# The last 96-row tile of gate and up: from seven products of 96 rows to seven of 64 rows and a plain 32 + 32, in 64-column matmuls

## The chip, the cores and the metric

The kernel runs on one core of a Trainium2 chip. Its engines each work through their own queue: TensorE (PE in the profile; its weight loads are shown as PEld), VectorE (DVE), ScalarE (ACT), GpSimd (POOL) and SyncE (SP), which issues most of the DMA transfers. The metric is the device time of one execution in microseconds (us); lower is better. Before the change it is 2099.88 us, the median of three runs (2099.81 to 2101.02).

## The reference

The input x has 8 batches of 1024 tokens with 512 features, all in float32. The tokens are normalised, and two branches are computed from them; their product is added to x.

```python
xn = _layernorm(x, axis=-1)
s = _L0_attn_ref(xn, ...)          # three decayed retrievals, gated, 128 wide
gate = einsum('bsh,oh->bso', xn, lut[gate_idx])     # 512 -> 1376
up   = einsum('bsh,oh->bso', xn, lut[up_idx])       # 512 -> 1376
h    = silu(gate) * up
g    = silu(einsum('bsh,oh->bso', h, lut[down_idx]))  # 1376 -> 512
return x + s * g
```

The weights of gate, up and down come from a table of 16 values by integer indices. 1376 = 10 x 128 + 96, so that gate and up have a last tile of 96 rows. The change concerns this tile.

## The kernel before, in words

**Two phases.** Phase 1 (`phase_1`) normalises and transposes the tokens, computes the retrieval branch batch by batch, and builds the weights from the indices on the side. It writes what phase 2 needs to device memory: the weights, already with the sums that the products below need, and for each batch in `xs_d` the transposed tokens and their sums. Phase 2 (`phase_2`) runs over the 8 batches. For each it computes h with the products of gate and up (`quads` for ten tiles, `single` for the last), and then `down`.

**Seven products for eight.** Gate and up are multiplied in blocks of two by two. The 1024 tokens of a batch form two halves: quarters 0 and 2 are one, quarters 1 and 3 the other. The 512 features form two halves too, and gate and up stand one over the other. Instead of eight block products there are seven, on sums and differences of weight blocks (s1 to s4) and of token blocks (t1 to t4). The products' results are combined by copies in PSUM and by additions. Token blocks are b11 and b21 (first token half, first and second feature half), b12 and b22 (second token half). Products 1 to 3 use b11, b21 and b22 themselves, products 4 to 7 sums. b12 itself is used by no product.

**The stage `single` (L831).** Product k has two matmuls (L845), one for each 128 features, with 96 columns of weights and 512 tokens. It uses four PSUM banks: pc (s21), pb (s12), pa (s11) and pe (sE). They show as `fs` and `fsE` in the profile. The order is:

- product 1 into pa; ScalarE copies pa to u2 (L855)
- product 6 into pb; VectorE adds: u2 = pb + u2 (L857), the first addition
- `at_last(5)`: five sums for the stage that follows
- ScalarE copies u2 into pc (L859)
- product 5 into pe; ScalarE copies pe to e (L861)
- product 2 onto pa; ScalarE takes Silu of it (L863)
- product 7 onto pc; VectorE adds: u3 = pc + e (L865), the second addition
- `at_last(1)`: one more sum
- product 3 onto pe; VectorE and ScalarE make Silu of pe + u2 (L868, L869)
- product 4 onto pc; VectorE multiplies by the first Silu (L871); GpSimd multiplies the other half (L872)

The temporary tile t, with u2, u3, e and the Silu, lies in the room "u2" of the pool `tmp` in batch 0, and in the room "e5" of `tmp2` in the others.

**The order around it.** In batch 0 `single` comes before `quads`. There the hook `at_last` is `sums_beside`, which has GpSimd make sums of tokens (L828). In batches 1 to 7 `single` comes after `quads` and before `down`, and `at_last(n)` calls `vector_sums` (L1119, L1123): n of the sums of blocks of h that `down` needs for its first nodes, on VectorE. Ten are planned: four of 128 x 512 into z, four of 128 x 1024 and two of 128 x 512 into sx and sy.

**`quads`** works in nodes (`Node`, L874): two groups of four tiles with seven nodes each, then three nodes for the last pair of tiles, (1, 6), (5, 7) and (2, 3), and `Fourth` (L926), the fourth products of the last pair. Each node loads its weights into one of three ring buffers. After the node (4, 4) of a group, GpSimd multiplies h by a tile u3 and then by a tile e5 (`multiply`, L992 to L994). `restore` (L965) loads the second quarter of a token block again where sums have overwritten it.

**Queues.** `keep_order` ties the instructions of PE, DVE, ACT and POOL to the order of the source, engine by engine. SyncE's order comes from the scheduler; a load that waits for its room holds up those behind it on that queue.

**Phase 1's part.** `features` (L485) writes the token blocks of a half batch to `xs_d` (L520, L525, L531), and `gate_up` (L257) builds a tile's weights: three index loads, a look-up on VectorE, four sums on GpSimd, and a write.

Of the kernel before, what the change touches and what calls it, by code (L numbers as in the profile page):

```python
# [9 lines left out]
F32 = mybir.dt.float32  # L10
# [38 lines left out]
def recurrent_block(ctx: ExitStack, tc, x, wq, wk, wv, wo, wg, decay_logits, out_scale, lut, gidx, uidx, didx, out):  # L49
# [38 lines left out]
    small = p_a = p_c = p_r = None  # L88


    wgu_d = [dram.tile([P, 14, m], F32, name=f"wgud{o}", tag=f"wgud{o}") for o, (_, m) in enumerate(OCH)]
# [154 lines left out]
    def ffn_weights(build, pool, pair_pool):  # L246
# [10 lines left out]
        def gate_up(o):  # L257
            s, m = OCH[o]
            n = 2 * NV * m
            idx = build.tile([P, NB], I32, name="idx", tag="idx", bufs=2)  # L260
            iv = idx[:, :n].rearrange("p (a b) -> p a b", b=m)
# [7 lines left out]
            w = wf[:, : 2 * n].rearrange("p (k two m) -> p k two m", two=2, m=m)  # L269
            a21, a11, a12, a22, s1, s2, s3, s4 = (w[:, k] for k in range(8))  # L270
# [4 lines left out]
            nc.gpsimd.tensor_tensor(s4, a12, s2, ALU.subtract)  # L275
            wide = wf[:, 2 * m : 2 * n].rearrange("p (a b) -> p a b", b=m)
            if o >= 4 * NQ:
                defer(3, lambda: nc.sync.dma_start(out=wgu_d[o], in_=wide))
            if o >= 2 * NK:
                return  # L280
# [106 lines left out]
    def project(b, pools, sides, kept):  # L387
# [97 lines left out]
        def features(hf):  # L485
# [48 lines left out]
            nc.scalar.copy(c11, pa)  # L534
# [254 lines left out]
    W_OF = {1: 0, 2: 1, 4: 2, 5: 3, 6: 4, 7: 5, 3: 6}  # L789
    X_OF = {1: 0, 2: 1, 3: 2, 5: 3, 6: 4, 7: 5, 4: 6}  # L790
    D_OF = {1: 0, 7: 1, 2: 2, 3: 3, 5: 4, 6: 5, 4: 6}
    ORDER = (1, 6, 5, 7, 2, 3, 4)

    def phase_2():
        with (
# [18 lines left out]

                return fx.tile([P, 7, 7, H], F32, name=f"xs{b}", tag="xs")

            def load_x(b, xs, first=0, end=7):
                nc.sync.dma_start(
                    out=xs[:, first:end, 0:4, :],
                    in_=xs_d[b][:, 2 * first : 2 * end].rearrange("p (k r) (s t) -> p k (r s) t", r=2, s=2),  # L820
                )

            def sums_of_x(xs):
# [4 lines left out]
                    nc.gpsimd.tensor_tensor(o, x1, x2, ALU.subtract)  # L828
                    yield

            def single(b, o, xs, h_tail, at_last, room):  # L831

                s, m = OCH[o]
                w = ring.tile([P, 14, P], F32, name=f"wr{b}_{o}", tag="wr")
                nc.sync.dma_start(out=w[:, :, :m], in_=wgu_d[o])
                ha, hb = h_tail[:m, :U], h_tail[:m, U:]


                pc, pb, pa, pe = (bank(r, f"f{r}{b}_{o}")[:m, :] for r in ("s21", "s12", "s11", "sE"))
                t = room.tile([P, 4, U], F32, name=f"t{b}_{o}", tag="e5" if room is tmp2 else "u2")  # L840
                u2, u3, e, sg = (t[:m, k, :] for k in range(4))

                def product(ps, k, start, stop):
                    for n in range(2):
                        nc.tensor.matmul(  # L845
                            ps,
                            lhsT=w[:, 2 * W_OF[k] + n, :m],
                            rhs=xs[:, X_OF[k], 2 * n : 2 * n + 2, :],
                            start=start and n == 0,
                            stop=stop and n == 1,  # L850
                            skip_group_check=True,
                        )

                product(pa, 1, True, False)
                nc.scalar.copy(u2, pa)  # L855
                product(pb, 6, True, True)
                nc.vector.tensor_tensor(u2, pb, u2, ALU.add)  # L857
                at_last(5)
                nc.scalar.copy(pc, u2)  # L859
                product(pe, 5, True, False)  # L860
                nc.scalar.copy(e, pe)  # L861
                product(pa, 2, False, True)
                nc.scalar.activation(sg, pa, AF.Silu)  # L863
                product(pc, 7, False, False)
                nc.vector.tensor_tensor(u3, pc, e, ALU.add)  # L865
                at_last(1)
                product(pe, 3, False, True)
                nc.vector.tensor_tensor(hb, pe, u2, ALU.add)  # L868
                nc.scalar.activation(hb, hb, AF.Silu)  # L869
                product(pc, 4, False, True)  # L870
                nc.vector.tensor_tensor(ha, pc, sg, ALU.mult)  # L871
                nc.gpsimd.tensor_tensor(hb, hb, u3, ALU.mult)  # L872

            class Node:  # L874

# [81 lines left out]
                def fifth_copy(self):  # L957
                    self.add()

            def quads(b, xs, h, sums, made, at_last):  # L960

                def restore(*ks):  # L965

                    some_of = slice(X_OF[ks[0]], X_OF[ks[-1]] + 1, max(X_OF[ks[-1]] - X_OF[ks[0]], 1))
                    there = xs_d[b].rearrange("p (k r) t -> p k r t", r=2)
                    nc.scalar.dma_start(out=xs[:, some_of, 1, :], in_=there[:, some_of, 0, H:])

                def two(ap):
                    return ap.rearrange("p (a t) -> p a t", a=2)
# [86 lines left out]
                def every():  # L1059
                    for q in range(NQ):  # L1060
                        for ks, empty, after in steps(q):
                            yield Node(b, q, ks, xs), empty, after
                    for ks, empty, after in pair_steps():
# [304 lines left out]
            more = iter(())  # L1368
            xs = room_for_x(0)
            for k in (1, 6, 5, 2, 7, 3, 4):  # L1370
                load_x(0, xs, X_OF[k], X_OF[k] + 1)
            for b in range(B):
                h = hp.tile([P, 2 * NK, T], F32, name=f"h{b}", tag="h")
                h_tail = hp.tile([P, T], F32, name=f"ht{b}", tag="ht")
# [25 lines left out]
                quads(b, xs, h, more, made, no_sums if b else at_last)  # L1400
                if b == 0:
                    hold(out=wd_tail[: OCH[-1][1], :], in_=wdt_d)
                else:
                    single(b, NO - 1, xs, h_tail, at_last, tmp2)
                nodes_done = [0]

                def beside(k):
# [8 lines left out]
                    load_x(b + 1, xs, X_OF[ORDER[n]], X_OF[ORDER[n]] + 1)  # L1416
                    if n > 4:
                        some(more, 4)

# [47 lines left out]
```

## Time and profile before

| what | us |
|---|---|
| median of three runs (lowest, highest) | 2099.88 (2099.81, 2101.02) |
| span of the profiled execution | 2099.0 |
| mean granted clock of TensorE, share of full speed | 1.000 |
| TensorE busy in it | 2084.7 |
| TensorE busy with the matmuls of `single` (L845), 8 batches | 102.7 |
| VectorE, ScalarE, GpSimd busy in the span | 1441.1, 944.3, 1042.0 |
| distance from one batch's `single` to the next | 188.3 |

The profile is one execution, and its span runs from the first to the last instruction; the runs' times are a little longer. A group line names the source line, the engine, the operation, the tiles written and read (out<-in), the shape and the count. After the bar stand busy time, the mean length of one in nanoseconds, and the engine's idle time just before, with what ended it. Matmuls are pipelined, so a record is longer than the distance to the next one. The matmuls of the stage, by their two groups of PSUM banks:

```profile
L845 PE MATMUL fs<-xs,wr 128*96 128x512 f32 x160 | 72.6, 592 | 0.4 <-ACT bl L685 0.4
...
L845 PE MATMUL fsE<-xs,wr 128*96 128x512 f32 x64 | 30.1, 592 | 0.0
```

160 + 64 records are two for each of the 14 matmuls of the 8 batches; they are busy for 72.6 + 30.1 = 102.7 us, and the idle time ahead of them is 0.4 us in all.

### The profile page before, as it was taken

Reading aid. Unit: us, or ns where it says so; the run is one execution under the profiler, and the core shown is the slowest. Engines: PE = TensorE matmul, PEld = TensorE weight load, DVE = VectorE, ACT = ScalarE, POOL = GpSimd, SP = SyncE. Lnnn points to the kernel's source line nnn. Section 1 sums busy time; section 2 is a strip of 40 time slices with the busy share of each in tenths; the row PEclk is TensorE's granted clock in tenths of the full one; section 3 lists DMA queues with packets and bytes.
Section 4 is the critical chain, followed back from the end, with each engine's and each line's share of the span. In section 5 each row is a group of like instructions: output and inputs, shape, how many; then the busy total and the mean of one; then the engine's idle time right before and its main releaser. Section 6 shows DMA issues by size and latency. Waiting matters only on the chain.

```text
span 2099.0 us, 32182 instructions
## 1 busy us (share of the span) xinstructions
PE 2084.7 (99%) x11691; PEld 1751.2 (83%) x11691; DVE 1441.1 (69%) x2214; ACT 944.3 (45%) x2116; POOL 1042.0 (50%) x1050
## 2 busy tenths in 40 slices
PE   9999999999999999999999999999999999999999
PEld 7887888888878888797878888787988888797877
DVE  8889998879458765675557457556755665675567
ACT  4766676676435324423531442344144224414531
POOL 4554665354365456527443751664275265527432
PEclk9999999999999999999999999999999999999999
DMA  8766769654754734554464446445544634464442
GB/s 219 146 180 164 201 156 203 166 155 133 204 180 158 257 131 153 167 216 146 159 219 151 161 150 235 145 144 194 188 148 151 249 128 158 152 233 145 146 157 105
DMA packets 184347, 359.68 MB, mean 171 GB/s; under 512 B 50895, under 2 KB 122206, under 8 KB 184190
## 3 DMA queue, kind: packets, MB, share of 16 engines
q1 hardware_dynamic: 168742, 330.61, 51.4%
q10 hardware_dynamic: 10968, 12.34, 1.9%
q0 software_dynamic: 4480, 14.68, 1.7%
q8 instruction: 93, 1.52, 0.3%
q14 instruction: 64, 0.52, 0.1%
HBM read 281.95 MB, written 75.63 MB: 170 GB/s over the span
## 4 chain that ended last, share of the span: by engine, by line
PE 81%; DVE 2%; DMA 2%; POOL 0%; issue 0%; ACT 0%; SPq 0%; DVEq 0%; ACTq 0%
PE s L897 33%; PE sE L897 6%; PE s12d L1155 5%; PE s21d L1155 5%; PE s11d L1155 5%; PE fs L845 3%; PE pd L1273 3%; PE ps L1280 3%; PE pv L444 2%; PE sEd L1155 2%; PE po L684 2%; PE fsE L845 1%; PE s11d L1166 1%; PE s21d L1166 1%; PE s12d L1166 1%; PE sEd L1166 1%
## 5 line engine op out<-in xcount | busy, mean ns | idle before, releaser
L897 PE MATMUL s<-xs,wq 128*128 128x256 f32 x3264 | 731.5, 379 | 1.0 <-DVE s L920 1.0
L897 PEld LDWEIGHTS s<-xs,wq 128*128 128x128 f32 x3264 | 619.4, 190 | 97.3 <-issue 8.4
L920 DVE TENSOR_TENSOR s<-s,e 128x512 f32<-128x512 f32 x136 | 95.1, 700 | 190.0 <-ACT s L919 190.0
L1244 POOL TENSOR_TENSOR cu<-cu 128x256 f32<-128x256 f32 x32 | 35.1, 1096 | 306.5 <-DVE cl L1243 306.5
L444 PE MATMUL pv<-wvg_sb,xnT 128*128 128x387 f32 x512 | 177.4, 488 | 0.0
L828 POOL TENSOR_TENSOR xs<-xs 128x256 f32<-128x256 f32 x224 | 171.4, 791 | 6.8 <-PE fs L845 2.3
L924 DVE TENSOR_TENSOR sE<-s,e 128x512 f32<-128x512 f32 x136 | 95.1, 699 | 103.6 <-PE s L897 103.5
L990 POOL TENSOR_TENSOR u<-u,e 128x512 f32<-128x512 f32 x64 | 81.7, 1298 | 146.6 <-DVE u L986 114.4
L915 ACT COPY e<-sE 128x512 f32<-128x512 f32 x136 | 79.7, 586 | 139.7 <-PE sE L897 139.7
L897 PE MATMUL sE<-xs,wq 128*128 128x256 f32 x544 | 139.6, 379 | 0.0
L444 PEld LDWEIGHTS pv<-wvg_sb,xnT 128*128 128x128 f32 x512 | 94.2, 190 | 53.7
L994 POOL TENSOR_TENSOR h<-h,u 128x512 f32<-128x512 f32 x64 | 81.0, 1290 | 109.0 <-DVE u L1001 109.0
L423 POOL TENSOR_SCALAR rstd<-rstd 128x1 f32<-128x1 f32 x56 | 27.8, 496 | 204.1 <-ACT junk L422 203.0
L908 ACT COPY s<-s 128x512 f32<-128x512 f32 x136 | 77.5, 570 | 109.5 <-PE s L897 106.1
L919 ACT COPY s<-s 128x512 f32<-128x512 f32 x136 | 77.5, 570 | 97.4 <-PE s L897 97.4
L1155 PE MATMUL s12d<-wdd,z 128*128 128x128 f32 x896 | 118.5, 275 | 0.6 <-ACT s12d L1177 0.6
L897 PEld LDWEIGHTS sE<-xs,wq 128*128 128x128 f32 x544 | 103.4, 190 | 14.1
L1155 PEld LDWEIGHTS s12d<-wdd,z 128*128 128x128 f32 x896 | 109.0, 192 | 0.8 <-ACT s12d L1177 0.8
L224 DVE TENSOR_SCALAR leaf<-idx,lut_x,lut_sb 128x1024 int32<-128x1024 int32 (+2 forms) x119 | 108.0, 932 | 0.0
L641 POOL TENSOR_TENSOR qb<-ga,q_tab 128x384 f32<-128x384 f32 x56 | 77.8, 1389 | 54.3 <-DVE ga L637 36.7
L241 DVE COPY_PREDICATED leaf<-bit,leaf 128x1024 f32<-128x1024 uint8 (+2 forms) x68 | 92.2, 1356 | 1.7
L1284 POOL TENSOR_TENSOR gx<-gx,cu 128x512 f32<-128x512 f32 x32 | 40.7, 1277 | 82.0 <-DVE cu L1282 64.5
(266 smaller groups left out, 4521.6 us busy)
## 6 DMA issues: line engine op xcount, KB each, us to landing
wq<-quadd SPq DMA_DIRECT2D x112, 896.0 KB, 4.6
wdd<-wdd SPq DMA_DIRECT2D x56, 896.0 KB, 4.7
xs<-xsd SPq DMA_DIRECT2D x56, 512.0 KB, 6.7
wq<-quadd SPq DMA_DIRECT2D x48, 448.0 KB, 4.2
x<-in_x SPq DMA_DIRECT2D x64, 256.0 KB, 7.7
xsd<-ts SPq DMA_DIRECT2D x16, 1024.0 KB, 14.1
gx<-in_x SPq DMA_DIRECT2D x64, 256.0 KB, 5.5
out<-gx POOLq DMA_DIRECT2D x56, 256.0 KB, 2.3
```

The costliest lines, as they stand in the source:

```text
L224: nc.vector.tensor_scalar(o.bitcast(I32), iv, lut_x[:rows, k, :], lut_i[:rows, k, 0:1], ALU.bitwise_and, ALU.bitwise_xor,)
L241: nc.vector.copy_predicated(o, bits[level - 1][:rows, :n], t[:rows, :n])
L444: nc.tensor.matmul(pv, lhsT=xnT[:, v, ts(c, P)], rhs=wvg_sb[:, v, :], start=(v == 0), stop=(v == NV - 1))
L828: nc.gpsimd.tensor_tensor(o, x1, x2, ALU.subtract)
L845: nc.tensor.matmul(ps, lhsT=w[:, 2 * W_OF[k] + n, :m], rhs=xs[:, X_OF[k], 2 * n : 2 * n + 2, :], start=start and n == 0, stop=stop and n == 1,
L897: nc.tensor.matmul(self.t[n][:, ts(a, H)], lhsT=self.w[:, a, (0, 1, 6, 3, 4, 5, 2)[i - 1], :], rhs=self.xs[:, X_OF[self.ks[a]], D_OF[i], : ...
L920: nc.vector.tensor_tensor(self.t[1], self.t[1], self.e, ALU.add)
L924: nc.vector.tensor_tensor(self.t[3], self.t[2], self.e, ALU.add)
L990: nc.gpsimd.tensor_tensor(o[:, n], o[:, n], other[:, n], ALU.add)
L994: nc.gpsimd.tensor_tensor(of_h(half, n), of_h(half, n), two(other[:, n]), ALU.mult)
L1155: nc.tensor.matmul(self.t[n][:, ts(a, P)], lhsT=self.lhs[i][:, e, ts(a, P)], rhs=self.w[:, e, D_OF[i], :], start=start and a == 0 and e == ...
L1166: nc.tensor.matmul(self.t[n][:, ts(a, P)], lhsT=self.left[:, ts(2 * (n // 2) + a, P)], rhs=wd_left[:, D_OF[self.k], ts(n % 2, P)], start=F ...
```

## The change

The 96 rows are split. The first 64 rows of gate and up still go by seven products (`MS = 64`), now with 64 columns of weights. The last 32 rows of each (`MR = 32`) are computed plainly: one set of 64 weight columns holds the 32 gate rows and the 32 up rows, and goes over all four feature blocks of 128 for both token halves (`others`). That needs b12 itself, which phase 1 now writes to `xs_d` as well (16 blocks instead of 14) and which `room_for_single` loads into the tile t.

Each product has four matmuls instead of two: for each 128 features one with the first 256 tokens, whose results go to PSUM partitions 0 to 63, and one with the other 256, whose results go to partitions 64 to 127. In `others` each matmul has 512 tokens; one token half goes to partitions 0 to 63, the other to 64 to 127. The weights lie in one array (`wgld`).

The order in `single` becomes 1, 5, others, 6, 2, 7, 3, 4, with new copies and additions. In batches 1 to 7 the load of b12 is traced ahead of the node (5, 7), in batch 0 just ahead of `single`. On SyncE's queue as built it stands behind the loads of the nodes' weights and ahead of those of `Fourth` and of `single`; in batch 0 it stands behind the first node's weights.

```diff
+    MS = 64
+    MR = OCH[-1][1] - MS
+    wgl_d = dram.tile([P, 14 * MS + 8 * MR], F32, name="wgld", tag="wgld")
...
-    xs_d = [dram.tile([P, 14, U], F32, name=f"xsd{b}", tag=f"xsd{b}") for b in range(B)]
+    xs_d = [dram.tile([P, 16, U], F32, name=f"xsd{b}", tag=f"xsd{b}") for b in range(B)]
...
+            if m < P:
+                right = idx[:, 2 * NV * MS : n].rearrange("p (c two b) -> p c two b", two=2, b=MR)
+                for two, src in enumerate((gidx, uidx)):
+                    nc.sync.dma_start(
+                        out=right[:, :, two, :], in_=src[:, s + MS : s + m].rearrange("(c p) b -> p c b", p=P)
+                    )
+                m = MS
...
-            nc.sync.dma_start(out=there[:, 4:6, :], in_=b22)
+            nc.sync.dma_start(out=there[:, 4:8, :], in_=xnT[:, :, ts(2 * hf + 1, H)])
...
-            defer(2, lambda: nc.sync.dma_start(out=there[:, 6:14, :], in_=ts_.rearrange("p a b u -> p (a b) u")))
+            defer(2, lambda: nc.sync.dma_start(out=there[:, 8:16, :], in_=ts_.rearrange("p a b u -> p (a b) u")))
...
+            def room_for_single(b, room):
+                t = room.tile([P, 4, U], F32, name=f"t{b}", tag="e5" if room is tmp2 else "u2")
+                nc.sync.dma_start(out=t[:, 0:2, :], in_=xs_d[b][:, 4:6, :])
+                return t
+
+            def single(b, xs, h_tail, at_last, t):
+                w = ring.tile([P, 14, P], F32, name=f"wr{b}", tag="wr").rearrange("p a b -> p (a b)")
+                nc.sync.dma_start(out=w[:, : 14 * MS + 8 * MR], in_=wgl_d)
+                s21, s12, s11, sE = (bank(r, f"f{r}{b}")[:, :H] for r in ("s21", "s12", "s11", "sE"))
+                rest = bank("s11", f"fr{b}")
+                e, sg, sr = t[:, 2, :H], t[:, 2, H:], t[:, 3, :]
+                parts = [slice(MS * c, MS * (c + 1)) for c in range(2)]
+
+                def product(ps, k, start=False):
+                    for n in range(2):
+                        at = MS * (2 * W_OF[k] + n) + (8 * MR if W_OF[k] > 2 else 0)
+                        for c, part in enumerate(parts):
+                            nc.tensor.matmul(
+                                ps[part],
+                                lhsT=w[:, at : at + MS],
+                                rhs=xs[:, X_OF[k], 2 * n + c, :],
+                                start=start and n == 0,
+                                stop=False,
+                                skip_group_check=True,
+                            )
+
+                def others():
+                    x_of = [[xs[:, X_OF[k], 2 * n : 2 * n + 2, :] for k in (1, 2) for n in range(2)]]
+                    x_of.append([t[:, n, :] for n in range(2)])
+                    x_of[1] += [xs[:, X_OF[3], 2 * n : 2 * n + 2, :] for n in range(2)]
+                    for v in range(NV):
+                        for c, part in enumerate(parts):
+                            nc.tensor.matmul(
+                                rest[part],
+                                lhsT=w[:, 6 * MS + 2 * MR * v :][:, : 2 * MR],
+                                rhs=x_of[c][v],
+                                start=v == 0,
+                                stop=v == NV - 1,
+                                skip_group_check=True,
+                            )
+
+                def to_h(half, ps, gate):
+                    for c, part in enumerate(parts):
+                        nc.vector.tensor_tensor(
+                            h_tail[:MS, half * U + c * H :][:, :H], ps[part], gate[part], ALU.mult
+                        )
+
+                product(s11, 1, True)
+                nc.scalar.copy(s12, s11)
+                product(sE, 5, True)
+                nc.scalar.copy(e, sE)
+                others()
+                for c in range(2):
+                    g, u = (slice(MS * c + MR * k, MS * c + MR * (k + 1)) for k in range(2))
+                    nc.scalar.activation(sr[u], rest[g], AF.Silu)
+                product(s12, 6)
+                nc.scalar.copy(s21, s12)
+                nc.vector.tensor_tensor(s12, s12, e, ALU.add)
+                at_last(5)
+                product(s11, 2)
+                nc.scalar.activation(sg, s11, AF.Silu)
+                product(s21, 7)
+                nc.vector.tensor_tensor(sE, s21, e, ALU.add)
+                at_last(1)
+                for c in range(2):
+                    u = slice(MS * c + MR, MS * (c + 1))
+                    nc.vector.tensor_tensor(h_tail[MS : MS + MR, ts(c, U)], rest[u], sr[u], ALU.mult)
+                product(s12, 3)
+                nc.scalar.activation(e, s12, AF.Silu)
+                product(s21, 4)
+                to_h(0, s21, sg)
+                to_h(1, sE, e)
...
+                    pair = pair_steps()
+                    for ks, empty, after in pair:
+                        if ks == (5, 7):
+                            of_single()
...
-                    single(b, NO - 1, xs, h_tail, sums_beside, tmp)
+                    single(b, xs, h_tail, sums_beside, room_for_single(b, tmp))
...
+                def of_single():
+                    if b:
+                        ahead.append(room_for_single(b, tmp2))
...
-                    single(b, NO - 1, xs, h_tail, at_last, tmp2)
+                    single(b, xs, h_tail, at_last, ahead[0])
```

Below, the second addition is the one of s21 and e into sE, and the first the one of s12 and e into s12.

More of the change, by code (lines that the diff above doesn't have):

```diff
@@ L88, in recurrent_block @@
     small = p_a = p_c = p_r = None
-    wgu_d = [dram.tile([P, 14, m], F32, name=f"wgud{o}", tag=f"wgud{o}") for o, (_, m) in enumerate(OCH)]
+    MS = 64
+    MR = OCH[-1][1] - MS
+    wgu_d = [dram.tile([P, 14, m], F32, name=f"wgud{o}", tag=f"wgud{o}") for o, (_, m) in enumerate(OCH[:-1])]
+    wgl_d = dram.tile([P, 14 * MS + 8 * MR], F32, name="wgld", tag="wgld")
     quad_d = [
@@ L260, in gate_up @@
             idx = build.tile([P, NB], I32, name="idx", tag="idx", bufs=2)
-            iv = idx[:, :n].rearrange("p (a b) -> p a b", b=m)
+            if m < P:
[5 more added lines that the diff above has]
+                m = MS
+            iv = idx[:, : 2 * NV * m].rearrange("p (a b) -> p a b", b=m)
             gs, us = (src[:, s : s + m].rearrange("(c p) b -> p c b", p=P) for src in (gidx, uidx))
@@ L268, in gate_up @@
             yield from look_up(build, wf[:, :n], idx[:, :n], P, n)
-            w = wf[:, : 2 * n].rearrange("p (k two m) -> p k two m", two=2, m=m)
-            a21, a11, a12, a22, s1, s2, s3, s4 = (w[:, k] for k in range(8))
+            if m < P:
+                w = [wf[:, ts(k, 2 * m)] for k in range(4)] + [wf[:, n + k * 2 * m :][:, : 2 * m] for k in range(4)]
+                a21, a11, a12, a22, s1, s2, s3, s4 = w
+            else:
+                w = wf[:, : 2 * n].rearrange("p (k two m) -> p k two m", two=2, m=m)
+                a21, a11, a12, a22, s1, s2, s3, s4 = (w[:, k] for k in range(8))
             nc.gpsimd.tensor_tensor(s1, a21, a22, ALU.add)
@@ L275, in gate_up @@
             nc.gpsimd.tensor_tensor(s4, a12, s2, ALU.subtract)
+            if m < P:
+                defer(3, lambda: nc.sync.dma_start(out=wgl_d, in_=wf[:, 2 * m : n + 8 * m]))
+                return
             wide = wf[:, 2 * m : 2 * n].rearrange("p (a b) -> p a b", b=m)
@@ L278, in gate_up @@
                 defer(3, lambda: nc.sync.dma_start(out=wgu_d[o], in_=wide))
-            if o >= 2 * NK:
-                return
             if o % 2 == 0:
@@ L791, in recurrent_block @@
     D_OF = {1: 0, 7: 1, 2: 2, 3: 3, 5: 4, 6: 5, 4: 6}
+    XD_OF = {1: 0, 2: 1, 3: 3, 5: 4, 6: 5, 7: 6, 4: 7}
     ORDER = (1, 6, 5, 7, 2, 3, 4)
@@ L815, in room_for_x, with load_x @@
                 return fx.tile([P, 7, 7, H], F32, name=f"xs{b}", tag="xs")
-            def load_x(b, xs, first=0, end=7):
+            def load_x(b, xs, k):
                 nc.sync.dma_start(
-                    out=xs[:, first:end, 0:4, :],
-                    in_=xs_d[b][:, 2 * first : 2 * end].rearrange("p (k r) (s t) -> p k (r s) t", r=2, s=2),
+                    out=xs[:, X_OF[k], 0:4, :],
+                    in_=xs_d[b][:, ts(XD_OF[k], 2)].rearrange("p r (s t) -> p (r s) t", s=2),
                 )
@@ L829, in sums_of_x @@
                     yield
[L831 to L843, printed above, removed]
-                    for n in range(2):
[L845 to L851, printed above, removed]
-                        )
[L854 to L857, printed above, removed]
-                at_last(5)
[L859 to L865, printed above, removed]
-                at_last(1)
[L867 to L872, printed above, removed]
@@ L958, in fifth_copy, with quads, some_of @@
                     self.add()
-            def quads(b, xs, h, sums, made, at_last):
+            def quads(b, xs, h, sums, made, at_last, of_single):
                 def restore(*ks):
-                    some_of = slice(X_OF[ks[0]], X_OF[ks[-1]] + 1, max(X_OF[ks[-1]] - X_OF[ks[0]], 1))
+                    def some_of(at):
+                        return slice(at[ks[0]], at[ks[-1]] + 1, max(at[ks[-1]] - at[ks[0]], 1))
                     there = xs_d[b].rearrange("p (k r) t -> p k r t", r=2)
-                    nc.scalar.dma_start(out=xs[:, some_of, 1, :], in_=there[:, some_of, 0, H:])
+                    nc.scalar.dma_start(out=xs[:, some_of(X_OF), 1, :], in_=there[:, some_of(XD_OF), 0, H:])
                 def two(ap):
@@ L1062, in every @@
                             yield Node(b, q, ks, xs), empty, after
-                    for ks, empty, after in pair_steps():
+                    pair = pair_steps()
+                    for ks, empty, after in pair:
+                        if ks == (5, 7):
+                            of_single()
                         yield Node(b, NQ, ks, xs), empty, after
@@ L1370, in phase_2 @@
             for k in (1, 6, 5, 2, 7, 3, 4):
-                load_x(0, xs, X_OF[k], X_OF[k] + 1)
+                load_x(0, xs, k)
             for b in range(B):
@@ L1397, in phase_2 @@
                     some(more, 2)
-                    single(b, NO - 1, xs, h_tail, sums_beside, tmp)
+                    single(b, xs, h_tail, sums_beside, room_for_single(b, tmp))
                 made = left_weights(sp, wd_left) if b == 0 else iter(())
-                quads(b, xs, h, more, made, no_sums if b else at_last)
+                ahead = []
+                def of_single():
+                    if b:
+                        ahead.append(room_for_single(b, tmp2))
+                quads(b, xs, h, more, made, no_sums if b else at_last, of_single)
                 if b == 0:
@@ L1415, in beside @@
                         more = sums_of_x(xs)
-                    load_x(b + 1, xs, X_OF[ORDER[n]], X_OF[ORDER[n]] + 1)
+                    load_x(b + 1, xs, ORDER[n])
                     if n > 4:
```

## The prediction

> **What bounds the kernel now.** The first part of the page first, for the busiest engine; then the chain that ended last, for what the end hangs on.
>
> ```profile
> PE 2084.7 (99%) x11691; PEld 1751.2 (83%) x11691; DVE 1441.1 (69%) x2214; ACT 944.3 (45%) x2116; POOL 1042.0 (50%) x1050
> ...
> PE 81%; DVE 2%; DMA 2%; POOL 0%; issue 0%; ACT 0%; SPq 0%; DVEq 0%; ACTq 0%
> ```
>
> TensorE (PE) is busy for all but 14 us of 2099.0, at a granted clock of 1.000. A stage therefore costs what its matmuls take, plus any wait that the change puts between them. Next the timeline of TensorE through the changed stage in batch 1 (start, length, engine, line, tiles, count; a float32 matmul of the source is recorded as two).
>
> ```profile
> 881.88 3.60 PE L845 MATMUL fs<-xs,wr 128*96 128x512 f32 x8
> 885.31 1.88 PE L845 MATMUL fsE<-xs,wr 128*96 128x512 f32 x4
> 887.03 3.60 PE L845 MATMUL fs<-xs,wr 128*96 128x512 f32 x8
> 890.46 1.88 PE L845 MATMUL fsE<-xs,wr 128*96 128x512 f32 x4
> 892.18 1.88 PE L845 MATMUL fs<-xs,wr 128*96 128x512 f32 x4
> 893.89 1.05 PE L1155 MATMUL s11d<-wdd,h 128*128 128x128 f32 x8
> ```
>
> From 881.88 to 893.89 stand 28 records without a gap: 12.01 us, 0.429 us for each of 512 columns. All eight batches have such a stage; the other batches' timelines repeat these distances. VectorE (DVE) in the same stretch:
>
> ```profile
> 885.57 0.69 DVE L857 TENSOR_TENSOR t<-fs,t 96x512 f32<-96x512 f32 x1 [2.73 <-PE fs L845]
> 886.17 0.68 DVE L1123 TENSOR_TENSOR z<-h 128x512 f32<-128x512 f32 x1
> 886.89 1.10 DVE L1123 TENSOR_TENSOR z<-z,h 128x512 f32<-128x512 f32 x1
> 887.91 0.68 DVE L1123 TENSOR_TENSOR z<-h 128x512 f32<-128x512 f32 x1
> 888.51 0.68 DVE L1123 TENSOR_TENSOR z<-h,z 128x512 f32<-128x512 f32 x1
> 889.11 1.21 DVE L1123 TENSOR_TENSOR sx<-h 128x1024 f32<-128x1024 f32 x1
> 890.73 0.69 DVE L865 TENSOR_TENSOR t<-fs,t 96x512 f32<-96x512 f32 x1 [0.41 <-PE fs L845]
> ```
>
> The five L1123 sums for the next stage (`at_last(5)`) stand between the two additions of this stage. They end at 890.32, and VectorE then waits only 0.41 us for product 7. So the sums just fit under products 5, 2 and 7, which take 3 x 1.72 us.
>
> **The change, part by part.**
>
> Matmuls. Removed: 28 records of 512 columns, 12.01 us. Added: seven products of four matmuls with 256 columns, thus 56 records, and `others()`, eight matmuls with 512 columns, thus 16 records. All use 64 of the array's columns, in turns the left and the right half. The trace shows 256 columns at 0.216 us (one node's 28 records follow one another in 6.05 us, 782.61 to 788.66). No row shows two matmuls in two halves at once, so the price has two ends. If a left and a right one run together, a pair costs what one full-width matmul costs: 28 x 0.216 + 8 x 0.429 = 9.48 us. If they queue: 56 x 0.216 + 16 x 0.429 = 18.96 us. I take the first, because the nearest row is the 128-column matmul: two 64-column ones fill the same columns and stream the same number of tokens. As the two records of one matmul follow one another in the same half, the right half ends one slot (0.22 us) after the left.
>
> The Trainium skill, "TensorE: Matmul & The Clock Gate", Part 3, gives 2.38x measured for three column tiles, that is 79% of the ideal. As an estimate by that page, slots would be 1/0.79 as long and the matmuls alone would take 12.0 us, no gain; with the wait below, some 20 us over all batches would be lost. No row here shows column tiles side by side.
>
> Switching the array's tile width costs nothing in this trace: a transpose with 12 output columns stands between full-width matmuls.
>
> ```profile
> 27.04 1.89 PE L505 MATMUL pb<-ts,wqs 128*128 128x256 f32 x8
> 28.77 0.27 PE L473 MATMUL pg<-ident,g 128*12 128x128 f32 x1
> 28.88 2.77 PE L444 MATMUL pv<-wvg_sb,xnT 128*128 128x387 f32 x8
> ```
>
> 27.04 + 8 x 0.216 = 28.77, and 0.11 us for 128 columns: no gap on either side. The skill's "TensorEngine Tiling (Array Packing)", Key Properties, says that changing the tiling mode drains the engine. By the row the term is 0. By the rule, with the 0.16 us by which a 256-column record (0.379) outlasts its slot as an estimate, 16 switches would add 2.6 us.
>
> The new wait, batches 1 to 7. The order of VectorE's work is the order of the source, and `at_last(5)` still stands between the two additions. But product 5 and `others()` have gone ahead of it, so only products 2, 7 and 3 are left behind it, 3 x 0.86 = 2.6 us, and product 4 accumulates into s21, which the second addition must have read. From the stage's first matmul (0):
> - products 1 and 5: 1.73; others: 5.16, right half 5.59; product 6: 6.02.
> - ScalarE starts 0.25 us after the last matmul's slot (product 1 before: slots end at 883.60, copy at 883.85). Two Silus of 512 elements come before the copy s12 to s21 in its order: 5.84 + 2 x 0.58 (L998, two in 1.15) = 7.00. The copy of 256 elements takes 0.37 (L1188): 7.37. Product 7 waits for it, 0.57 us past product 2.
> - VectorE's addition: 7.40, next start 0.34 later (L1189, 897.21 to 897.55). The sums took 886.17 to 890.32 = 4.15; the 1.10 one was beside GpSimd, which by now is done, so 0.68: 3.73. From 7.74 to 11.47.
> - The second addition starts 0.08 before that record ends and takes 0.43: 11.82. Product 4 starts at 11.9 instead of 9.2, behind a 2.7 us gap; it ends at 12.76, its right half at 12.98.
>
> 12.98 against 12.01: +0.97 us. Were the Silus free, copy and all would move up 0.5 us: +0.5. Were the 1.10 us sum to stay: +1.4. Queued behind the waiting product 4 is the whole down stage. Behind the waiting addition on VectorE are one more sum (1.2), two products of 32 rows (0.6 each) and four of 64 x 256 (0.34 each). These end by 14.6, and `down` needs VectorE first 3.3 us after its start (893.89 to 897.21), at 16.3: covered. GpSimd loses the L872 product (1.27), off the path: nothing.
>
> Batch 0 has GpSimd sums in that place, so product 4 does not wait: 9.48 + 0.22 + 0.57 = 10.3. But its new load of b12 (512 KB) can go only when phase 1's last matmul lets its room go (about 584.2), and `others()` wants it 2.16 us after the start, at 586.62. Rows for its landing:
>
> ```profile
> xs<-xsd SPq DMA_DIRECT2D x56, 512.0 KB, 6.7
> ...
> wr<-wgud SPq DMA_DIRECT2D x8, 672.0 KB, 4.9
> ...
> bld<-bl ACTq DMA_DIRECT2D x8, 512.0 KB, 4.3
> ```
>
> 4.3 to 6.7 us; 6.7 is for seven in one burst, so I take 4.4: 588.6, a 2.0 us wait. 12.3 against 12.06 (584.46 to 596.52): +0.2, with ends -1.8 and +2.5.
>
> Loads in batches 1 to 7. The load of b12 into e5's room waits for GpSimd's last product with e5 and stands on SyncE's queue ahead of the loads of the fourth products' weights, which stand ahead of the stage's own:
>
> ```profile
> 864.98 4.95 POOL L994 TENSOR_TENSOR h<-h,e 128x512 f32<-128x512 f32 x4
> ...
> 868.28 0.80 SPq L933 DMA_DIRECT2D w<-wgud x2
> ```
>
> They go at about 870.4 instead of 868.3, land 2.8 us later (the row of DMA issues) or, behind 512 KB, 4 us, and are used at 875.64: 1.2 us to spare, price 0. If the cover is gone, each us late costs one, up to 7 over the batches. Phase 1 writes 256 KB more per half batch, 4 MB at the mean of 171 GB/s, in 580 us of matmuls: 0. The last tile's two extra index loads and smaller GpSimd sums lie under the same matmuls: 0.
>
> Sum: 7 x 0.97 + 0.2 = +7.0 us. The profiled execution has a span of 2099.0 us and the median is 2099.88, so 0.9 lies around it: 2106.0 and **2107 us**, slower by 0.33%. Ends: 7 x 0.5 - 1.8 = +1.7 and 7 x 1.4 + 2.5 = +12.3, with late weight loads +19: 2101.5 to 2119.
>
> **Rivals.**
>
> *The halves queue.* For it: no row shows them together. Against: weight loads already overlap matmuls (PEld busy 83%). Then products 2, 7 and 3 take 5.2 us and cover the 4.5 us of VectorE work; 18.96 - 12.01 = +6.95 us, eight times: 2155.
>
> *They overlap in part*, say with slots a quarter longer: `others()` ends 1.4 us later, product 4 and its right half take 0.3 more, so 0.97 becomes 2.7 us, in all eight some 22: about 2122. For it and against it the trace has no row.
>
> *The wait does not bind.* For it: a wait for several events is put down to one, and the change's addition could be passed by if VectorE took the sums after it. Against: order and read-before-write above. It decides only if the addition is done by 9.2. Then 9.48 + 0.22 + 0.57 saves 1.74 in each of seven, 12 us, or 2.31 without the Silus' delay: 2084 to 2088, faster.
>
> **How the numbers follow.** Forecast 0.78, own range 2101 to 2114; halves queue 0.12; in part 0.06; wait does not bind 0.04. A measurement tells 0.2%, 4.2 us, from no change: of the forecast's 0.78, 0.14 falls within it. Faster 0.04, same 0.14, slower 0.82. The range leaves out the two far cases (0.16): 2098 to 2123.
>
> **What would show it.** In the changed profile: left and right 64-column matmuls starting in pairs, some 0.43 us per pair of 256 columns; a gap of 2 to 3 us on TensorE ahead of product 4, put down to VectorE's second addition; no such gap in batch 0, but one in `others()` for a DMA; no gap ahead of the fourth products. It is wrong if pairs start one after another, if product 4 follows product 3 without a gap, or if stages outside move by more than 1 us.

## The result and the profile after

The changed kernel takes 2114.3 us, median of four runs (2114.02 to 2116.03), beside 2100.45 us, median of four (2099.81 to 2101.06), for the kernel before. The ratio is 1.0067, with a 95% interval of 1.0053 to 1.0082. The side was right, but the loss is 14 us instead of 7: the time lies 0.3 us above the forecast's own range (2101 to 2114) and inside the outer one (2098 to 2123). The profiled execution, the longest of the four, has a span of 2113.9 us, 14.9 us more than before; the other three span 2111.9 to 2112.2. First the page's busy times and its chain:

```profile
PE 2080.8 (98%) x12043; PEld 1761.5 (83%) x12043; DVE 1445.0 (68%) x2246; ACT 943.3 (45%) x2132; POOL 1026.2 (49%) x1042
...
PE 91%; DVE 6%; DMA 1%; ACT 1%; issue 1%; SPq 0%; POOL 0%; DVEq 0%; ACTq 0%
```

TensorE is busy for 3.9 us less, and VectorE now has 6% of the chain instead of 2%. Next the waits of TensorE in the changed kernel (for what, us in total, times, longest):

```profile
PE fs L870 <- DVE fsE L915: 17.6, 7, 2.5
...
PE fr L885 <- DMA t<-xsd: 1.3, 1, 1.3
...
PE fr L885 <- DMA xs<-xsd: 0.9, 1, 0.9
```

The wait for the second addition (L915) is there seven times, once in each of batches 1 to 7, and 2.5 us long each time. The two waits for a DMA in `others()` are single ones, in batch 0 and in batch 7. Then TensorE's timeline through the changed stage in batch 1, and the end of the stage in batch 4 (start, length, engine, line, tiles, count, idle time before and its releaser):

```profile
880.28 1.03 PE L949 MATMUL s<-xs,wq 128*128 128x256 f32 x4
881.23 1.08 PE L870 MATMUL fs<-xs,wr 128*64 128x256 f32 x8
882.15 1.03 PE L870 MATMUL fsE<-xs,wr 128*64 128x256 f32 x8
883.01 0.59 PE L885 MATMUL fr<-xs,wr 128*64 128x512 f32 x1
883.02 0.59 PE L885 MATMUL fr<-t,wr 128*64 128x512 f32 x1
...
886.44 3.78 PE L870 MATMUL fs<-xs,wr 128*64 128x256 f32 x32
892.74 1.93 PE L870 MATMUL fs<-xs,wr 128*64 128x256 f32 x8 [2.52 <-DVE fsE L915]
894.60 1.93 PE L1212 MATMUL s11d<-wdd,h 128*128 128x128 f32 x8
...
1464.57 1.08 PE L870 MATMUL fs<-xs,wr 128*64 128x256 f32 x8 [2.52 <-DVE fsE L915]
1465.59 1.16 PE L1212 MATMUL s11d<-wdd,h 128*128 128x128 f32 x8
```

In `others()` the two halves' matmuls start 0.01 us apart, and a product's 8 records take 0.86 to 0.92 us: left and right run together. After the gap, though, the eight records of product 4 take 1.93 us in batch 1 and 1.08 in batch 4, with the same gap before them. The first node of `down` is stretched too, 1.93 against 1.16. The stage is 13.37 us long in batch 1 (881.23 to 894.60) and 12.53 in batch 4 (1453.06 to 1465.59). Windows over batch 1 (stretch, its length, then busy time and count of PE, PEld, DVE, ACT and POOL, the granted clock, the DMA share, GB/s) show why:

```profile
881.20:890.20 9.00, 9.00 (x65) 4.41 (x64) 2.70 (x7) 3.31 (x8) 4.86 (x7) 1.00 0.61 233
890.20:892.70 2.50, 0.03 (x2) 0.00 (x0) 2.50 (x5) 0.00 (x0) 0.00 (x0) 1.00 0.00 0
892.70:894.60 1.90, 1.86 (x9) 0.72 (x9) 1.86 (x3) 0.38 (x1) 0.00 (x0) 0.54 0.00 0
894.60:896.37 1.77, 1.77 (x11) 1.77 (x9) 1.71 (x4) 0.00 (x0) 0.00 (x0) 0.53 0.43 65
896.37:898.20 1.83, 1.83 (x19) 1.83 (x18) 0.61 (x2) 0.73 (x2) 0.00 (x0) 1.00 0.94 374
```

During the gap TensorE does nothing and VectorE is busy all the time. Then the granted clock is about half until 896.3, for some 3.4 us, and full again after that. What VectorE does in the gap, in its own timeline of the changed kernel:

```profile
888.26 0.43 DVE L910 TENSOR_TENSOR fs<-fs,t 128x256 f32<-128x256 f32 x1 [6.16 <-ACT fs L909]
888.60 0.68 DVE L1180 TENSOR_TENSOR z<-h 128x512 f32<-128x512 f32 x1
...
891.13 1.22 DVE L1180 TENSOR_TENSOR sx<-h 128x1024 f32<-128x1024 f32 x1
892.27 0.42 DVE L915 TENSOR_TENSOR fsE<-fs,t 128x256 f32<-128x256 f32 x1
```

The five sums of `at_last(5)` run from 888.60 to 892.3, between the two additions, and the second addition releases product 4.

**The sum over the program.** From one batch's stage to the next it is 188.29 us before. After, five of the six distances from batch 1 to batch 7 are 190.59 to 190.62 and one, after batch 4, is 189.00 (1453.06 to 1642.06): 12.3 us more together. From the start of the last stage to the end it is 90.6 us (2023.26 to 2113.9) instead of 87.4: +3.25, of which 0.91 is the DMA wait. Up to batch 1's stage the changed kernel is 0.65 us ahead. 12.3 + 3.25 - 0.65 = 14.9.

### The profile page after: what moved, and what is told of

Its sections match the earlier page's. It is cut to its first block, busy times and chain, and to the rows that moved or that the text cites. A ratio compares the mean times of both kernels' runs of the same rounds, so it can differ in the third digit from the quotient of the medians.

```text
span 2113.9 us, 32896 instructions
## 1 busy us (share of the span) xinstructions
PE 2080.8 (98%) x12043; PEld 1761.5 (83%) x12043; DVE 1445.0 (68%) x2246; ACT 943.3 (45%) x2132; POOL 1026.2 (49%) x1042
## 4 chain that ended last, share of the span: by engine, by line
PE 91%; DVE 6%; DMA 1%; ACT 1%; issue 1%; SPq 0%; POOL 0%; DVEq 0%; ACTq 0%
PE s L949 33%; PE pv L459 7%; PE sE L949 6%; PE s11d L1212 5%; PE s12d L1212 5%; PE s21d L1212 5%; PE po L699 3%; PE pd L1330 3%; PE ps L1337 3%; PE sEd L1212 2%; PE pe L520 2%; PE pc L520 2%; PE pa L520 2%; PE psc L675 2%; PE pu L685 2%; PE fr L885 1%
## 5 line engine op out<-in xcount | busy, mean ns | idle before, releaser
L1048 POOL TENSOR_TENSOR h<-h,e 128x512 f32<-128x512 f32 x64 | 81.2, 1305 | 0.0
```

The lines of the kernel that those rows point to most:

```text
L1048: nc.gpsimd.tensor_tensor(of_h(half, n), of_h(half, n), two(other[:, n]), ALU.mult)
```

## The experiments

The theory after the result: VectorE's sums make the gap, and the gap costs twice, by its length and by the clock after it. The rivals: the 64-column matmuls themselves are slower or lower the clock; or the new wait has another cause, so that moving the sums doesn't help. A time without an interval is that of a single execution.

**1. `others()` under the sums.** The eight plain matmuls and their Silus go from ahead of product 6 to behind the first addition's sums in the order of the source.

```diff
                 nc.scalar.copy(e, sE)
-                others()
-                for c in range(2):
-                    g, u = (slice(MS * c + MR * k, MS * c + MR * (k + 1)) for k in range(2))
-                    nc.scalar.activation(sr[u], rest[g], AF.Silu)
                 product(s12, 6)
                 nc.scalar.copy(s21, s12)
                 nc.vector.tensor_tensor(s12, s12, e, ALU.add)
                 at_last(5)
+                others()
+                for c in range(2):
+                    g, u = (slice(MS * c + MR * k, MS * c + MR * (k + 1)) for k in range(2))
+                    nc.scalar.activation(sr[u], rest[g], AF.Silu)
```

> The changed kernel with others() moved behind product 6, its copy, the first addition and the five sums, so that others() and products 2, 7 and 3 (6.0 us) lie between the two additions instead of 2.6 us. Theory (VectorE's sums are late for product 4, and the gap that follows lowers TensorE's clock for some us): no gap ahead of product 4 in batches 1 to 7, granted clock 1.00 throughout, the stage 9.8 to 9.9 us there and about 10.7 in batch 0, where b12 is still awaited: 2084 us, 16 below the kernel before. Rival (64-column matmuls themselves lower the clock): the clock still falls to half after the stage, some 1.6 us in each batch: about 2095. Rival (something behind the stage takes the time): the time stays near 2114.

Measured: 2087.4 us (2086.14 to 2087.95), ratio to the kernel before 0.9938 (0.9925 to 0.9952); the same instructions as in the changed kernel, 27 us faster than it. TensorE's timeline of this kernel in batch 1:

```profile
886.09 1.89 PE L885 MATMUL fr<-xs,wr 128*64 128x512 f32 x8
887.81 3.74 PE L870 MATMUL fs<-xs,wr 128*64 128x256 f32 x32
891.48 1.16 PE L1212 MATMUL s11d<-wdd,h 128*128 128x128 f32 x8
```

The last four products, 32 records, follow `others()` without a gap, and `down` follows them at full clock. The stage takes 9.75 us (from 881.73), and the distance between stages is 186.22 us, 2.07 less than before. So the order of the sums against the plain matmuls decides the sign of the whole change. The time is 3 us above the 2084 expected; about half of that has come by the end of batch 0's stage, which starts 0.95 us later than in the kernel before and takes 11.20 us instead of 10.7. The other half was not traced to a stage.

**2. The sums behind the second addition.** The same five sums, later on VectorE.

```diff
                 nc.vector.tensor_tensor(s12, s12, e, ALU.add)
-                at_last(5)
...
                 nc.vector.tensor_tensor(sE, s21, e, ALU.add)
+                at_last(5)
                 at_last(1)
```

> The changed kernel with the five sums moved behind the second addition; the matmuls' order stays. Theory: the 2.5 us gap ahead of product 4 goes, and the stage takes some 10.3 us. VectorE then ends its sums and the products for h_tail at about 16.5 us after the stage's start, where the down stage wants its first addition at 13.6 to 14.5: part of the gap, 0 to 2 us, comes back in the down stage. 2088 if the down stage hides it, up to 2105 if it does not or if the clock falls there too. Rival (sums are not what product 4 waits for): 2114.

Measured: 2098.04 us (2096.64 to 2099.32), ratio 0.9987 (0.9978 to 0.9996). The timeline of TensorE in batch 1:

```profile
887.73 4.65 PE L870 MATMUL fs<-xs,wr 128*64 128x256 f32 x40
892.30 1.16 PE L1212 MATMUL s11d<-wdd,h 128*128 128x128 f32 x8
...
897.05 1.16 PE L1212 MATMUL s11d<-wdd,sx 128*128 128x128 f32 x8 [0.46 <-ACT cl L1293]
...
899.60 1.16 PE L1212 MATMUL s12d<-wdd,z 128*128 128x128 f32 x8 [0.50 <-DVE s12d L1246]
```

The stage has no gap (882.51 to 892.30 = 9.79 us, 2.22 less than before), but the distance between stages falls by only 0.54 us. The other 1.7 us come back in `down`, two waits of some 0.5 us among them. The second is for VectorE's addition (L1246), which now comes behind the sums; the profile puts the first down to a copy on ScalarE (L1293), and why that one comes late is open. The work that makes the gap can't simply be put off; it has to run under matmuls that don't need it.

**3. The kernel before with a longer `at_last`.** It keeps the 96-column matmuls, but has nine sums between the additions, so that product 4 gets a gap of the same length.

```diff
-                at_last(5)
+                at_last(9)
```

> The kernel before, full-width matmuls only, with nine sums instead of five between the two additions: VectorE is some 3.9 us later with the second one, so that product 4 waits some 2.6 us in batches 1 to 7. Theory (an idle stretch of TensorE of that length lowers the clock, whatever the matmuls' width): the clock falls to half for some us after the gap in most batches, each batch loses about 2.6 + 1.6 us, less what the down stage saves on VectorE: about 2127. Rival (the clock falls because the half-width matmuls load the array less): the gap alone, clock 1.00: about 2117.

Measured: 2126.49 us in one execution. TensorE's timeline of this kernel in batch 1 (512-column records):

```profile
891.32 1.88 PE L845 MATMUL fsE<-xs,wr 128*96 128x512 f32 x4
895.85 3.42 PE L845 MATMUL fs<-xs,wr 128*96 128x512 f32 x4 [2.65 <-DVE t L865]
899.10 1.05 PE L1155 MATMUL s11d<-wdd,h 128*128 128x128 f32 x8
```

Product 4's four records take 3.42 us instead of 1.88, after a gap of 2.65 us. In this way the granted clock falls after three of the seven gaps and not after the other four. The distance between stages is 191.18 us from a batch whose clock stays up to the next, and 192.6 to 192.8 from one whose clock falls: again some 1.5 us for the fall. So it belongs to the gap, and the 64-column matmuls are not its cause. That the total comes so near the expected 2127 is partly luck: the clock falls in three batches instead of most, and the gap's length costs 2.9 us (191.18 - 188.29) instead of 2.6. The distances tell the theory from its rival; the total alone would not.

**4. The gap filled.** The changed kernel, with three full-width matmuls of 512 tokens into a free PSUM bank between products 3 and 4 in batches 1 to 7. Nothing reads them; the second addition comes as late as in the changed kernel.

```diff
+                if b:
+                    spare = bank("s12", f"sp{b}")
+                    for n in range(3):
+                        nc.tensor.matmul(
+                            spare,
+                            lhsT=w[:, :P],
+                            rhs=xs[:, X_OF[4], 0:2, :],
+                            start=n == 0,
+                            stop=n == 2,
+                            skip_group_check=True,
+                        )
                 product(s21, 4)
```

> The changed kernel with three full-width matmuls of 512 columns, whose result nobody reads, between products 3 and 4 in batches 1 to 7: 6 x 0.429 = 2.57 us of work that fills the gap; product 4 still waits for VectorE. Theory (the gap lowers the clock): clock 1.00, product 4 starts no later, and the time falls by the clock's part, 1.6 us in six batches: about 2104.5. Rival (the half-width matmuls lower the clock): about 2114. Rival (the extra work delays product 4): above 2114.

Measured: 2107.88 us (2107.33 to 2109.6), ratio 1.0037 (1.0023 to 1.005). The timeline of TensorE in batch 1:

```profile
889.49 3.78 PE L870 MATMUL fs<-xs,wr 128*64 128x256 f32 x32
893.21 2.84 PE L925 MATMUL sp<-xs,wr 128*128 128x512 f32 x6
895.98 1.08 PE L870 MATMUL fs<-xs,wr 128*64 128x256 f32 x8
896.99 1.16 PE L1223 MATMUL s11d<-wdd,h 128*128 128x128 f32 x8
```

Product 4 comes 11.70 us after the stage's start, 0.19 later than in the changed kernel, as the three matmuls and the changes of width around them take a little more than the gap; but it takes 1.08 us, and the mean granted clock of the execution is 1.000 instead of 0.995. More work makes the kernel 6.4 us faster. The distance between stages is 189.18, 0.89 more than in the kernel before: the price of the late product 4 without the clock, with the 0.19 in it. The total is 3.4 us above what was expected. Of that, 2.9 us lie ahead of batch 0's stage, which starts at 586.85 here and at 583.93 in the changed kernel; in the six experiments this start lies between 585.27 and 586.85, though none of them edits phase 1. The 0.19 us in seven batches are another 1.3.

**5. The halves one after the other.** Both loops are turned, so that all matmuls of the left half stand ahead of all of the right in a product, and in `others()`.

```diff
-                    for n in range(2):
-                        for c, part in enumerate(parts):
+                    for c, part in enumerate(parts):
+                        for n in range(2):
...
-                    for v in range(NV):
-                        for c, part in enumerate(parts):
+                    for c, part in enumerate(parts):
+                        for v in range(NV):
```

> The changed kernel with the two loops exchanged: within a product, and within others(), all matmuls of the left half come first, then all of the right half. Theory (matmuls start in the order of the source, a left and a right one run together only where they are neighbours): of a product's 8 records only one left-right neighbour pair overlaps at each change of side, so a product takes 6 slots of 0.216 us instead of 4, others() 14 of 0.429 instead of 8: the stage some 16 us in batches 1 to 7, 15 in batch 0, about 2135 us (2130 to 2146, by whether the clock falls behind the remaining gap of 1 to 1.5 us). Rival (the hardware finds the other half's matmul wherever it stands in the queue): near 2114.

Measured: 2126.34 us in one execution, less than the 2130 to 2146 expected. TensorE's timeline of this kernel in batch 1:

```profile
884.81 1.08 PE L870 MATMUL fsE<-xs,wr 128*64 128x256 f32 x8
885.67 2.31 PE L885 MATMUL fr<-xs,wr 128*64 128x512 f32 x5
887.39 0.64 PE L885 MATMUL fr<-t,wr 128*64 128x512 f32 x1
887.82 0.59 PE L885 MATMUL fr<-xs,wr 128*64 128x512 f32 x1
...
897.16 1.84 PE L870 MATMUL fs<-xs,wr 128*64 128x256 f32 x8 [2.47 <-DVE fsE L915]
```

A product still takes 0.86 us, as if its halves stood in turns: the four right-half records start beside the four left-half ones that stand ahead of them. In `others()`, with eight ahead of eight, the right half (`t`) starts 1.72 us after the left (885.67 to 887.39), which is four slots of 0.43. So a matmul for the other half starts while up to four records that stand ahead of it are still to be done, and only `others()` pays for the order. Product 4 starts 13.27 us after the stage's start instead of 11.51, behind a gap of the same length; the clock falls after three of the seven. The expectation had let every product pay for the order.

**6. Four sums instead of five.** One sum goes from the first hook to the second.

```diff
-                at_last(5)
+                at_last(4)
...
-                at_last(1)
+                at_last(2)
```

> The changed kernel with four sums between the two additions and two after, instead of five and one: the gap ahead of product 4 is shorter by one 128x1024 sum, 1.13 us, some 1.4 us instead of 2.5. If a gap of that length leaves the clock alone, both parts go: 2114.3 - 7 x 1.1 - 6 x 1.6 = about 2097. If it lowers the clock as the longer one does: about 2106. If the share of batches with a lowered clock falls with the gap's length: between the two.

Measured: 2100.35 us (2098.8 to 2101.16), ratio 0.9996 (0.9987 to 1.0006), no difference from the kernel before that can be told. TensorE's timeline of this kernel in batch 1:

```profile
888.40 3.79 PE L870 MATMUL fs<-xs,wr 128*64 128x256 f32 x32
893.57 1.08 PE L870 MATMUL fs<-xs,wr 128*64 128x256 f32 x8 [1.39 <-DVE fsE L915]
894.59 1.16 PE L1212 MATMUL s11d<-wdd,h 128*128 128x128 f32 x8
```

A gap of 1.39 us leaves the clock alone in all seven batches. The distance between stages is 187.87 us (once 188.57), 2.7 less than in the changed kernel where its clock falls: 1.1 for the shorter gap, 1.6 for the clock. The total is 3 us above the 2097 expected for this case; 2.1 of them lie ahead of batch 0's stage (585.98 against 583.93 in the changed kernel).

**When the clock falls.** Read in windows of 0.2 us, the granted clock of the changed kernel is at a half for one stretch of 3.4 us after each of six gaps, starting from 0.1 to 1.2 us after the gap's end. The stretches end at 896.25, 1087.40, 1278.54, 1657.42, 1848.57 and 2039.70 us. The Trainium skill, "TensorE: Matmul & The Clock Gate", Part 1, says that the gate watches freely running windows of 3413 ns. The ends agree: their distances are 56.0, 56.0, 111.0, 56.0 and 56.0 times 3.4133 us, and those of the experiments 3 and 5 are whole multiples too (225.0 and 56.0; 168.0 and 169.0). With the edges of the windows known, each gap can be cut at them. Worked out for all gaps above 2 us (the longer part of a gap inside one window):

| kernel | clock falls, longest idle part of one window (us) | clock stays |
|---|---|---|
| changed | 2.52, 2.52, 2.24, 2.52, 2.43, 2.52 | 1.71 |
| experiment 3 | 2.22, 2.02, 2.37 | 1.92, 1.96, 1.99, 1.86 |
| experiment 5 | 2.47, 2.20, 1.94 | 1.44, 1.82, 1.36, 1.50 |

The clock falls when some 2.0 us of one window are idle (the bounds, 1.94 and 1.99, overlap by less than the windows of 0.2 us can tell), and then for the whole next window. Whether a gap of 2.5 us meets that hangs on where the window's edge cuts it: batch 4 was spared because an edge cut its gap into 0.81 and 1.71 us. The bound is read from the same 21 gaps that it explains, those of experiments 3 and 5 from one execution each; no further run tested it.

## Why the prediction was right in its side and wrong in its size

**Matmuls: right.** Left and right run together, as taken: pairs start 0.01 us apart, and stages without a wait take 9.75 us (experiment 1) and 9.79 (experiment 2), against 9.48 for the matmuls. That the forecast's 9.48 + 0.22 comes so near is luck. Its 0.22 us for a right half that ends a slot after the left isn't there, since the right half's records start beside the left's; a part of what stands in its place is the next term, which it put at 0. The rivals "the halves queue" (2155 us) and "overlap in part" (2122) fell.

**Switching the tile width: small, not nothing.** On the way in, the stage starts 0.09 us after the slots ahead of it end (880.28 + 4 x 0.216 = 881.14, against 881.23), and the first product takes 0.92 us where the second takes 0.86. On the way out, `down` starts some 0.1 us after product 4's slots end, and its first eight records last 1.16 us instead of the 1.05 before. That makes some 0.15 us on the way in and 0.2 on the way out, 0.2 of it outside the stage. In experiment 2 the eight records behind each of the two waits in `down` last 1.16 us too, so that a part of it may be the price of any stop. The Trainium skill's rule in "TensorEngine Tiling (Array Packing)", Key Properties, was nearer than the row with the 12-column transpose: the 0.16 us that the prediction worked out by it as an estimate stands against these 0.15 and 0.2.

**The new wait: the right mechanism, mis-sized, and this is the step that failed.** The order was as described, and the releaser was the second addition. Its length was even a little overrated: 2.52 us instead of 2.7, as the Silus of `others()` began 5.43 us after the start (886.66) and not at 5.84. The copy behind the Silus held product 7 up by less than forecast, too: some 0.16 us instead of 0.57, by the 3.78 us of products 6, 2, 7 and 3 (16 slots of 0.216 and the 0.16 by which the last record outlasts its slot make 3.62). Where the clock stays up, the stage takes 12.53 us (batch 4), not 12.98, as the gap is shorter and the right half's 0.22 us isn't there; with the switches outside the stage the distance grows by 0.7 us. With the gap filled it grows by 0.89; the term was 0.97. What the term lacked is what follows: it priced an idle TensorE at the time it is idle, with every matmul after it at the rates of a trace whose clock was 1.000 throughout. In six of seven batches the clock then fell to half for 3.4 us, and the distance grew by 2.3 instead of 0.7: 1.6 us more each, 9.7 us over the six. In batch 1 half of it lies in product 4 (13.37 - 12.53 = 0.84), and the other half in the first node of `down` (1.77 from 894.60 to 896.37, instead of 0.99). Experiments 3, 4 and 6 show it from three sides: a gap of much the same length between 96-column matmuls lowers the clock, the same delay without an idle TensorE doesn't, and half the gap doesn't.

The prediction did not weigh its own gap of 2.7 us against the page on the clock gate. That page, in Part 1, has the clock fall after at least one idle window of about 3.4 us. Taken by the letter it would have said that 2.7 us do nothing; here some 2.0 us inside one window were enough.

**Batch 0: right in the sum, with errors on both sides.** `others()` wanted b12 1.8 us after the start (585.71) and not after 2.16, as the right half starts beside the left. The right half began at 587.99, so that it waited 2.3 us instead of 2.0; TensorE was idle for 1.26 of them, as two records of the left half ran alone ahead. The 0.22 us of the right half isn't there. The stage takes 12.11 us (583.93 to 596.04) instead of the forecast 12.3 and the 12.06 before.

**Loads in batches 1 to 7: right but once.** There is no gap ahead of the fourth products in any batch. In batch 7 `others()` waits 0.91 us for a block of tokens that `restore` loads again, a load that the prediction did not weigh.

**The rival "the wait does not bind"** gave 2084 to 2088 us. It is not what the change does, but experiment 1, which takes the wait away by another order, measured 2087.4.

## What to carry to other kernels

When a stage on the busiest engine gets shorter, look at what another engine did under it between two of its own steps in that stage: that work doesn't get shorter with it, and a wait takes the place of the gain. Put work that needs nothing (here the plain matmuls) between the sums' start and the step that waits for what comes after them, rather than ahead of both. Here gaps on TensorE of 2.47 to 2.65 us cost another 1.5 to 1.6 us by the clock in 12 of 21 cases, and gaps of 1.39 us in none of seven, so a gap is worth shortening or filling even where the wait itself stays. Whether it helps to cut one in two was not tried.

## What the runs showed of the hardware that was not expected

- An idle part of some 2.0 us in one window of 3.413 us is enough to halve the granted clock for the next window, which costs 1.5 to 1.6 us where TensorE sets the end. The windows run freely, so the same gap of 2.52 us did it in six of seven batches and one of 2.65 us in three of seven; one of 1.39 us did it in none.
- A matmul for one half of the array starts beside one for the other half though up to four records that stand ahead of it are still to be done (experiment 5: the first right-half record at 887.39, while the left half's eight follow one another from 885.67 every 0.43 us). The Trainium skill, "TensorE: Matmul & The Clock Gate", Part 3, says that matmuls start and end strictly in order; the starts seen there do not agree with that.
- A change between 128-column and 64-column matmuls costs some 0.15 us on the way in and 0.2 on the way out.
- Three added matmuls that nothing reads, 7 x 3 in all, made the changed kernel 6.4 us faster, as TensorE is no longer idle there.
